# A four-layer graph network on one core: index layout, x loads, the place of the pair sums, ScalarE's order at batch norms and copies, and two basis groups moved

## The chip, the cores and the metric

The kernel runs on one core of one Trainium2 chip. The metric is the device time of one execution in microseconds (us). Lower is better. The core has TensorE (PE, matrix products into PSUM), VectorE (DVE), ScalarE (ACT), GpSimd (POOL) and SyncE (SP, here only a queue that issues DMAs). Each engine works through its own instructions in order, and waits on semaphores for what others produce.

## The reference, cut to what matters

Four graph layers follow one another on x (512 nodes, 512 features); each adds its output to x, and reads relu(layernorm(x)). All use one edge list of 16896 edges (`dst`, `src`), the last also a type of 0 or 1 for each edge.

```python
# layer 0: attention over the adjacency, 8 heads of 64, softmax over the heads for each pair of nodes
q, k, v = x @ Wq + bq, x @ Wk + bk, x @ Wv + bv              # each as (N, H, HEAD)
scores = einsum('nhd,mhd->nhm', q, k) / sqrt(HEAD)
scores = where(adj[:, None, :] == 0, -1e9, scores)
attn = softmax(scores, axis=1)                                # over the heads
out = einsum('nhm,mhd->nhd', attn, v) @ Wo + bo
h1 = layer_norm(x + out); y = layer_norm(h1 + relu(h1 @ W1 + b1) @ W2 + b2)
# layer 1: x = prelu(x @ lin_W.T + lin_b), then twice
h = x + segment_sum(x[src], dst)
h = prelu(h @ conv_W1[l].T + conv_b1[l]) @ conv_W2[l].T + conv_b2[l]
x = relu((h - mean) * rsqrt(var + eps) * gamma[l] + beta[l])  # mean and var over the nodes
# layer 2: degree-normalised sum of neighbours, a product, leaky relu
# layer 3: twice: w[r] = sum_b att[r, b] * basis[b] (2 relations, 30 bases of 512x512);
#          sum over the edges of sigmoid(x_j @ gate[r]) * x_j @ w[r], plus x @ root + bias
```

## The kernel before

A 512x512 matrix lies as four tiles of 128 rows. The edge list is turned into dense 512x512 count matrices, one for each edge type (`Bc`), and all four layers work with these.

**The start** (L115 to L464). The three index vectors are read as rows of 128 edges (132 chunks): 128 rows into `idx` and the last four into `idx2`, six DMAs, for `dst` and `src` on SP's queue and for the type on ScalarE's. Two tiles of x are loaded on ScalarE's queue, two on SP's, then the weights Wq and Wk on SP. GpSimd meanwhile sets constants, and issues loads of its own (L148, L150, L179). VectorE casts the indices to `kn` (L393); TensorE transposes them into `key`, so that an edge chunk is a column (L395 to L398). `look_for_strays` (L404) tests whether any edge lies outside its expected range, and leaves a flag; a branch on the flag follows on all engines (L461, L462). The first layer norm is made by `moments` (bn_stats and bn_aggr on VectorE, L342) and `first_norm` (L378: a square root on ScalarE, a reciprocal and a product on VectorE, then a ReLU with bias and scale on ScalarE), for one tile after the other. `flip` (L329) transposes the result on TensorE, and ScalarE copies it out of PSUM.

**The counting loop** (L723 to L740) runs over 204 entries of (count tile, group, chunk). For each chunk `rows_of` makes two one-hot tiles, `hd` on VectorE and `hs` on ScalarE (L548) or VectorE (L550), up to seven chunks ahead; `count` is a small product into a count tile's two PSUM banks. At the end of each of the four count tiles `counted` (L560) moves the banks out with ScalarE and VectorE. Between the counts stand other steps of TensorE at places that a plan (L693 to L719) computes from the string `line`: `p` is half of a 4-matmul product of the q, k and v projections, `G` is a basis group, `s` and `S` are scores of the first two attention blocks, `=` is the head sums of block 0. The bias copy of a projection comes some entries after its second half (`waits`).

**The attention** (L744 to L758) runs over 8 blocks (two halves of the query nodes, four tiles of key nodes). For a block: `scores` (L616: products, and a copy by ScalarE into `sc`, 128x2048), `shift` (L633: maximum over the heads, subtraction, VectorE; then the exponential, ScalarE, in place), `pairs` (L646: a sum of two pairs of heads, VectorE, tile `z`), `sums` (L652: head sums by TensorE into one PSUM bank), `weigh` (L657: reciprocal and scaling, VectorE), `values` (L662: products with v). In pass j the loop scales block j, adds the pairs of j+1, makes scores and shift of j+2, the values of j-1 and the sums of j+1.

**The basis groups** (L227). Part of the sums over the bases of layer 3 is made on TensorE: 40 groups of four matrices, 8 instructions each, from weights loaded by SP. Two groups in the first half of the work, three in the second, fill a PSUM bank; ScalarE copies the bank and stores it (L249, L250). There is one such bank. The other bases are accumulated by VectorE (L268). The string `USES` (L34) gives the order in which the loads are used, P for TensorE and V for VectorE.

**Order.** An instruction wrapped in `on` (or `keep`) stays in program order with the others so wrapped on its engine. The others are placed by a list scheduler. All VectorE and ScalarE work of the attention loop is wrapped; in the batch norms it isn't.

**Layer 1** (L938 to L1006). After an aggregate over the edges, four banks are copied, two by ScalarE and two by VectorE (L949 to L954), and a product follows. For each of four tiles, the second product is moved out by ScalarE with a bias (L981), statistics and a ReLU follow (L982 to L989), and `settle` (L827) transposes the tile.

Of the kernel before, what the change touches and what calls it, by code (L numbers as in the profile page):

```python
# [17 lines left out]
P = 128  # L18
# [12 lines left out]
RB = 4  # L31
STEPS = 2
BANKS = 8
USES = "P" * 26 + "VPVVVPPPPVVVPPPVVVVPPPPPPVVVVVVVVVVVV"  # L34
FEW = 4095
LESS = 2.0 ** -12
GW = 32
# [37 lines left out]
def gnn_kernel(ctx: ExitStack, tc: tile.TileContext, out: bass.AP, a: dict):  # L75
# [36 lines left out]
    raw = ExitStack()  # L112
    rp = raw.enter_context(tc.tile_pool(name="raw", bufs=1))

    idx = rp.tile([P, 3, P], I32, name="idx")  # L115
    idx2 = rp.tile([NCH - P, 3, P], I32, name="idx2")
    for i, name in enumerate(("dst", "src", "edge_type_2")):
        queue = (nc.sync, nc.sync, nc.scalar)[i]
        queue.dma_start(idx[:, i, :], a[name][0:P * P].rearrange("(c p) -> c p", p=P))
        queue.dma_start(idx2[:, i, :], a[name][P * P:E].rearrange("(c p) -> c p", p=P))  # L120
    x = const.tile([P, T, D], F32, name="x")
    for t in range(T):
        (nc.scalar, nc.sync)[t // 2].dma_start(x[:, t, :], a["x"][t * P:(t + 1) * P, :])
    ident = const.tile([P, P], F32, name="ident")
    make_identity(nc, ident)

# [97 lines left out]
    wide2 = const.tile([P, 32], F32, name="wide2")  # L224
    sums = []

    def basis_step(n=1):  # L227
        for _ in range(n):
            if len(done) == len(loads):
                return  # L230
            l, n, g = loads[len(done)]
            done.append(n)
            assert USES[bases.at] == "P"
            t = bases.take()
            if g == 0:
                sums[:] = [pbas.tile([P, 512], F32, tag="bas", name="bas")]
            if g < STEPS:
                k, at = FULL * NQ, 32 - 2 * NQ * (g + 1)
                lhsT = wide[l][:k, at:at + 32]
            else:  # L240
                k = STEPS * HALF_OF * NQ
                lhsT = wide2[:k, :]
            for j in range(RB):
                tc.keep_in_program_order(nc.tensor.matmul(  # L244
                    sums[0][32 * j:32 * j + 32, :], lhsT=lhsT,
                    rhs=t[:k, j, :], start=(g == 0), stop=(g == STEPS + l - 1)))
            if g == STEPS + l - 1:
                o = spool.tile([P, 512], F32, tag="sums", name="sums")
                nc.scalar.copy(o, sums[0])  # L249
                nc.scalar.dma_start(summed[l][n], o)  # L250

    def wrel_load(l, r, t):
# [134 lines left out]
    key = ep.tile([P, 4, NCH], F32, name="key")  # L387
    p = ps()
    pk = p[:, :3 * NCH].rearrange("p (i c) -> p i c", i=3)
    for ix, c0 in ((idx, 0), (idx2, P)):  # L390
        n = ix.shape[0]
        kn = rp.tile([n, 3, P], F32, name=f"kn{c0}")
        on(nc.vector.tensor_copy(kn, ix))  # L393
        for i in range(3):
            on(nc.tensor.transpose(pk[:, i, c0:c0 + n], kn[:, i, :], ident[:n, :n]))  # L395
    moments(mv4[:, 0, :], x[:, 0, :], on)
    on(nc.vector.tensor_copy(key[:, 0:2, :], pk[:, 0:2, :]))
    on(nc.vector.tensor_scalar(key[:, 2, :], pk[:, 2, :], 0.0, LESS, op0=ALU.is_equal, op1=ALU.max))  # L398

    stray = ep.tile([P, NCH], F32, name="stray")  # L400
    flag = const.tile([1, 1], I32, name="flag")
# [2 lines left out]
    def look_for_strays():  # L404
        over = rp.tile([P, NCH], F32, name="over")
        on(nc.vector.tensor_tensor(stray, key[:, 0, :], lim[:, 0, :], ALU.is_lt))
        on(nc.vector.tensor_tensor(over, key[:, 0, :], lim[:, 1, :], ALU.is_ge))
        on(nc.vector.tensor_add(stray, stray, over))
        some = rp.tile([P, 1], F32, name="some")
        on(nc.vector.tensor_reduce(some, stray, AX.X, ALU.max))  # L410
        p = ps()
        on(nc.tensor.matmul(p[0:1, 0:1], lhsT=some, rhs=ones, start=True, stop=True))
        on(nc.vector.tensor_copy(iot, it))
        on(nc.vector.tensor_scalar(key[:, 3, :], key[:, 1, :], -1.0, 0.5, op0=ALU.mult, op1=ALU.add))
        on(nc.vector.tensor_copy(flag, p[0:1, 0:1]))
        first_norm(0)
        moments(mv4[:, 1, :], x[:, 1, :], on)

    strayed = dram.tile([2, P, T * N], F32, name="strayed")

# [31 lines left out]

    look_for_strays()
    for t in range(2, T):
        moments(mv4[:, t, :], x[:, t, :], on)
        first_norm(t - 1)
    first_norm(T - 1)
    far_off = const.tile([P, P], BF16, name="far_off")
    on(nc.vector.tensor_scalar(far_off, ident, FAR, None, op0=ALU.mult))
    nc.gpsimd.memset(apart, 1.0)  # L460
# [223 lines left out]
    def advance(gen, n=1):  # L684
        for _ in range(n):
# [9 lines left out]
    shifts = [blocks[i].shift(2) for i in range(2)]  # L695
    takes = {"p": (8, lambda: advance(proj)), "G": (4, basis_step), "s": (6, lambda: advance(early[0])),
             "S": (6, lambda: advance(early[1])), "=": (12, lambda: blocks[0].sums())}
    line = "pppppGpppGpppGppGpppGssppGpGSSppGpGppGG="
    FIRST = 9
    ends = [n for n in range(len(order) - 1) if order[n + 1][0] > order[n][0]]  # L700
    whole = sum(takes[i][0] for i in line)
# [1 line left out]
    waits = None  # L703
    for i, what in enumerate(line):
        at = max(at, FIRST + (len(order) - 2 - FIRST) * passes // whole)
        at = next((e for e in ends if e - 6 < at <= e), at)
        if waits is not None:
            plan.setdefault(min(waits, at), []).append(lambda: advance(proj))
            waits = None
# [2 lines left out]
        if what == "p":  # L712
            halves += 1
            if halves % 2 == 0:
                waits = at + 4
        if line[:i + 1].count(what) == 2 and what in "sS":
            for step in range(3):
                plan.setdefault(at + 7 * step + 7, []).append(lambda j="sS".index(what): advance(shifts[j]))
# [23 lines left out]
        pass  # L742
    aoT = big("B")
    for j, block in enumerate(blocks):  # L744
        block.weigh()
        if j + 1 < len(blocks):
            blocks[j + 1].pairs()
        if j + 2 < len(blocks):
            for _ in blocks[j + 2].scores():
                pass  # L750
        if j:
            blocks[j - 1].values()
        if j + 1 < len(blocks):
            basis_step(2 if j < 4 else 1)
            blocks[j + 1].sums()
        if j + 2 < len(blocks):
            for _ in blocks[j + 2].shift():
                pass  # L758
# [61 lines left out]
    def exactly(emit):  # L820
# [3 lines left out]
        with branch.Else():  # L824
            emit(f32, 0)

    def settle(l, h2T, m, xn):  # L827

        if l == 0:
# [43 lines left out]
    for t in range(T):  # L873
# [8 lines left out]
        if t > 1:  # L882
            flip(y, t - 2, hT)
        transposed(t)
        basis_step(t % 2)
        if t < 2:
            advance(more)

# [49 lines left out]
    for l in range(2):  # L938
# [14 lines left out]
            else:  # L953
                on(nc.scalar.copy(aT[:, m, :], p))  # L954
        if l == 0:
            basis_step(2)
            advance(more, 3)
        else:
            advance(more, 2)
# [16 lines left out]
        for m in range(T):  # L976
            p = ps()
            product(p, [(w[:, k, ts(m)], h1T[:, k, :]) for k in range(T)])
            at = CB2 + T * l + m
            v = h2T[:, m, :]  # L980
            nc.scalar.activation(v, p, AF.Identity, bias=cols[:, at:at + 1])  # L981
            mean, rstd = stats(v)  # L982
            at = T * l + m
            sg = stat("sg")
            nc.vector.tensor_mul(sg, rstd, cols[:, GAM + at:GAM + at + 1])
            off = stat("off")
            nc.vector.tensor_mul(off, mean, sg)
            nc.vector.tensor_sub(off, cols[:, BET + at:BET + at + 1], off)
            nc.scalar.activation(v, v, AF.Relu, bias=off, scale=sg)  # L989
            if m > 1:  # L990
                settle(l, h2T, m - 2, xn)
            if m < 2:
                advance(more)
        if l == 0:
            basis_step(1)
            settle(l, h2T, 2, xn)
            basis_step(2)
            settle(l, h2T, 3, xn)
        else:
            basis_step(1)  # L1000
            settle(l, h2T, 2, xn)
            basis_step(1)
            settle(l, h2T, 3, xn)
            basis_step(1)
            gates = gate_rows(1, [apart.bitcast(F32).rearrange("p t n -> p (t n)")[:, N * r:N * r + N] for r in range(2)])
            next(gates)  # L1006
# [186 lines left out]
```

## Time and profile before

| | us |
|---|---|
| median of 3 runs | 525.57 (525.04 to 527.74) |
| profiled execution, its own time | 527.14 |
| its span | 525.3 |
| TensorE busy | 485.9 |
| VectorE busy | 402.4 |
| ScalarE busy | 196.6 |
| GpSimd busy | 37.4 |
| mean granted TensorE clock | 0.997 of full speed |
| first projection product (L479) starts | 21.17 |
| last values product (L670) ends | 189.4 |

An instruction's line in the profile is given as L and a number, that of the code above. A row of a timeline gives start, duration, engine, line, operation, output and input, a number of instructions, and in brackets the idle time of the engine before it and what ended it. A row of waits gives who waited for whom, the total in us, how often, and the longest. A row of windows gives a stretch and its length, the busy time of PE, weight loads, DVE, ACT and POOL with the numbers of instructions, the granted clock, the share of the DMA engines' time, and GB/s. Busy times of matmuls are modelled from their starts.

### The profile page before, as it was taken

Reading aid. Unit: us, or ns where it says so; the run is one execution under the profiler, and the core shown is the slowest. Engines: PE = TensorE matmul, PEld = TensorE weight load, DVE = VectorE, ACT = ScalarE, POOL = GpSimd, SP = SyncE. Lnnn points to the kernel's source line nnn. Section 1 sums busy time; section 2 is a strip of 40 time slices with the busy share of each in tenths; the row PEclk is TensorE's granted clock in tenths of the full one; section 3 lists DMA queues with packets and bytes.
Section 4 is the critical chain, followed back from the end, with each engine's and each line's share of the span. In section 5 each row is a group of like instructions: output and inputs, shape, how many; then the busy total and the mean of one; then the engine's idle time right before and its main releaser. Section 6 shows DMA issues by size and latency. Waiting matters only on the chain.

```text
span 525.3 us, 5734 instructions
## 1 busy us (share of the span) xinstructions
PE 485.9 (93%) x2014; PEld 248.7 (47%) x2014; DVE 402.4 (77%) x746; ACT 196.6 (37%) x318; POOL 37.4 (7%) x81
## 2 busy tenths in 40 slices
PE   1798999888999899999999899899699999999996
PEld 1333333334555545784444444644454475446642
DVE  6755477969889778999985597688649999999611
ACT  2786768753354212222421215224623610114000
POOL 6000000000000011110040000000010000000000
PEclk9999999998999999999999999999999999999999
DMA  7998777499896749959571794966932994530011
GB/s 229 267 226 220 189 188 171 118 257 230 208 213 165 156 94 262 288 186 238 128 234 67 243 233 121 365 152 169 251 70 80 305 274 167 171 145 2 0 41 41
DMA packets 43033, 94.06 MB, mean 179 GB/s; under 512 B 2124, under 2 KB 2520, under 8 KB 43000
## 3 DMA queue, kind: packets, MB, share of 16 engines
q1 hardware_dynamic: 34544, 67.77, 48.6%
q0 software_dynamic: 5712, 21.07, 13.9%
q10 hardware_dynamic: 2744, 4.79, 2.8%
q8 instruction: 20, 0.33, 0.3%
q14 instruction: 13, 0.11, 0.1%
HBM read 88.38 MB, written 5.24 MB: 178 GB/s over the span
## 4 chain that ended last, share of the span: by engine, by line
PE 66%; DVE 21%; ACT 9%; POOL 2%; issue 2%; ACTq 0%; POOLq 0%
PE pr L320 15%; PE acc L1101 10%; PE pg L320 7%; PE bas L244 4%; DVE wrel L268 4%; PE ps L479 4%; PE ps L655 4%; PE acc L1067 3%; PE ao L557 3%; ACT hs L548 2%; DVE st L344 2%; PE ps L492 2%; PE ao L670 2%; PE acc L918 2%; DVE sc L660 2%; PE psc L628 2%
## 5 line engine op out<-in xcount | busy, mean ns | idle before, releaser
L268 DVE SCALAR_TENSOR_TENSOR wrel<-basis,scal,wrel 128x1024 f32<-128x1024 f32 x60 | 74.2, 1283 | 1.9 <-DMA basis<-in_basis 1.9
L548 ACT ACTIVATE hs<-iot,key 128x512 f16<-128x512 f16 x75 | 49.1, 713 | 9.9 <-PE ao L557 8.2
L544 DVE TENSOR_SCALAR hd<-iot,key 128x32 f16<-128x32 f16 (+1 forms) x132 | 33.7, 294 | 21.6 <-PE ao L557 21.4
L244 PE MATMUL bas<-basis,wide 120*32 120x512 f32 (+1 forms) x320 | 43.3, 600 | 2.9 <-ACT sums L249 2.1
L268 DVE SCALAR_TENSOR_TENSOR w<-basis,scal,w 128x1024 f32<-128x1024 f32 x32 | 39.4, 1283 | 0.0
L557 PE MATMUL ao<-hs,hd 128*32 128x512 f16 x204 | 26.1, 395 | 3.5 <-DVE Bc L566 1.6
L479 PE MATMUL ps<-bigB,w 128*128 128x512 f32 x56 | 27.8, 618 | 1.0 <-ACT bigD L482 0.6
L352 ACT ACTIVATE sd<-mv,eps 128x1 f32<-128x1 f32 x28 | 8.1, 294 | 53.0 <-DVE mv L345 52.0
L644 ACT ACTIVATE sc<-sc 128x2048 f32<-128x2048 f32 (+1 forms) x10 | 15.7, 1566 | 22.4 <-DVE sc L643 22.3
L320 PE MATMUL pr<-bigE,w 128*128 128x512 f32 x48 | 21.4, 595 | 1.7 <-ACT bigE L954 1.7
L1149 DVE TENSOR_TENSOR u<-acc,x 128x512 f32<-128x512 f32 x4 | 2.8, 693 | 23.5 <-PE acc L1101 23.5
L320 PE MATMUL pr<-bigD,w 128*128 128x256 f32 x88 | 20.2, 380 | 0.0
L550 DVE TENSOR_SCALAR hs<-iot,key 128x512 f16<-128x512 f16 x57 | 20.1, 360 | 0.0
L557 PEld LDWEIGHTS <-hd 128*32 128x32 f16 x204 | 6.2, 94 | 27.5 <-issue 19.4
L630 ACT COPY sc<-psc 128x1024 f32<-128x1024 f32 x16 | 16.1, 1008 | 8.1 <-PE psc L628 8.1
L659 DVE RECIPROCAL rec<-ps 128x256 f32<-128x256 f32 x8 | 14.1, 1757 | 6.4 <-PE ps L655 6.4
L643 DVE TENSOR_TENSOR sc<-sc,half 128x2048 f32<-128x2048 f32 (+1 forms) x10 | 18.6, 1865 | 0.2
L660 DVE TENSOR_TENSOR sc<-sc,rec 128x2048 f32<-128x2048 f32 x8 | 18.3, 2292 | 0.3
L628 PE MATMUL psc<-bigC,bigD 64*128 64x256 f32 x128 | 18.2, 402 | 0.0
L320 PEld LDWEIGHTS pr<-bigD,w 128*128 128x128 f32 x88 | 16.6, 190 | 3.0 <-ACT bigE L863 0.8
L320 PE MATMUL pr<-w,bigE 128*128 128x512 f32 x40 | 17.8, 592 | 0.0
L492 PE MATMUL ps<-w,bigB 128*128 128x512 f32 x32 | 15.9, 618 | 2.0 <-DVE bigE L495 2.0
(312 smaller groups left out, 957.4 us busy)
## 6 DMA issues: line engine op xcount, KB each, us to landing
basis<-in_basis SPq DMA_DIRECT2D x32, 960.0 KB, 9.2
basis<-in_basis SPq DMA_DIRECT2D x23, 1024.0 KB, 9.6
basis<-in_basis SPq DMA_DIRECT2D x16, 448.0 KB
summed<-sums ACTq DMA_DIRECT2D x16, 256.0 KB, 7.2
w<-in_W POOLq DMA_DIRECT2D x4, 1024.0 KB, 7.0
row<-in_rows POOLq DMA_DIRECT2D x12, 256.0 KB, 9.6
wrel<-summed POOLq DMA_DIRECT2D x4, 512.0 KB, 7.9
w<-in_conv_W1T POOLq DMA_DIRECT2D x2, 1024.0 KB, 5.7
```

Of the source, the lines that this page charges most:

```text
L244: tc.keep_in_program_order(nc.tensor.matmul(sums[0][32 * j:32 * j + 32, :], lhsT=lhsT, rhs=t[:k, j, :], start=(g == 0), stop=(g == STEPS + ...
L268: on(nc.vector.scalar_tensor_tensor(to[r][:, i:i + 2, :], t[:, i:i + 2, :], scal[:, at:at + 1], to[r][:, i:i + 2, :], op0=ALU.mult, op1=AL ...
L320: nc.tensor.matmul(p, lhsT=lhsT, rhs=rhs, start=(i == 0), stop=(i == len(pairs) - 1))
L479: on(nc.tensor.matmul(p, lhsT=w[:, k, ts(m)], rhs=made["hT"][:, k, :], start=(k == 0), stop=(k == T - 1)))
L492: on(nc.tensor.matmul(p, lhsT=made["hT"][:, k, ts(t)], rhs=w[:, k, :], start=(k == 0), stop=(k == T - 1)))
L544: keep(nc.vector.tensor_scalar(hd[:, :w], iot[:, GW * groups_of[c][0]:GW * groups_of[c][0] + w], key[:, 0, c:c + 1], key[:, 2, c:c + 1], o ...
L548: keep(nc.scalar.activation(hs, iot, AF.Sign, bias=key[:, 3, c:c + 1]))
L557: keep(nc.tensor.matmul(cnt[b][GW * (g % T):GW * (g % T) + GW, :], lhsT=hd[:, at:at + GW], rhs=hs, start=(c == in_bank[g][b][0]), stop=(c ...
L628: on(nc.tensor.matmul(p[:, b, i, :], lhsT=kT[bs, 2 * q + i, ts(self.mt)], rhs=qT[bs, 2 * q + i, self.ns], start=False, stop=(i == 1)))
L655: on(nc.tensor.matmul(self.total, lhsT=ident, rhs=part, start=(j == 0), stop=(j == len(self.parts) - 1)))
L660: on(nc.vector.tensor_mul(self.sc, self.sc, rec[:, None, :].to_broadcast([P, H, NH])))
L1101: nc.tensor.matmul(self.out[t], lhsT=self.uT[r][:, k, ts(t)], rhs=wrel[r][:, k, :], start=False, stop=(r == 1 and k == T - 1))
```

## The change

The indices are read as 66 rows of 256 edges, three DMAs; the cast is made for one vector at a time, and each is transposed in two halves, to the even and the odd chunks. All of x is loaded on SP, ahead of the weights. Statistics and norm of tiles 0 and 1 come ahead of the stray test, statistics of tiles 2 and 3 inside it. In the plan, the snap to the end of a count tile reaches six entries to both sides, the bias copy comes two entries after its product, and the string's last part is changed. In the attention loop `pairs` of the next block comes ahead of `weigh`, and the second group of a pass ahead of the values. At the batch norms, the bias copy of tile m is kept ahead of the ReLU of tile m-1; at the first copy one group is issued, with its bank's copy kept in order. One group each is taken from the feed-forward's last tile and from that copy, and put at the end of each batch norm. `USES` follows.

```diff
-USES = "P" * 26 + "VPVVVPPPPVVVPPPVVVVPPPPPPVVVVVVVVVVVV"
+USES = "P" * 26 + "VPVVVPPVVVPPPPVVVVPPPPPPPVVVVVVVVVVVV"
...
-    idx = rp.tile([P, 3, P], I32, name="idx")
-    idx2 = rp.tile([NCH - P, 3, P], I32, name="idx2")
+    idx = rp.tile([NCH // 2, 3, 2 * P], I32, name="idx")
...
-        queue.dma_start(idx[:, i, :], a[name][0:P * P].rearrange("(c p) -> c p", p=P))
-        queue.dma_start(idx2[:, i, :], a[name][P * P:E].rearrange("(c p) -> c p", p=P))
+        queue.dma_start(idx[:, i, :], a[name].rearrange("(c p) -> c p", p=2 * P))
...
-        (nc.scalar, nc.sync)[t // 2].dma_start(x[:, t, :], a["x"][t * P:(t + 1) * P, :])
+        nc.sync.dma_start(x[:, t, :], a["x"][t * P:(t + 1) * P, :])
...
-    def basis_step(n=1):
+    def basis_step(n=1, keep=lambda ins: ins):
...
-                nc.scalar.copy(o, sums[0])
+                keep(nc.scalar.copy(o, sums[0]))
...
-    for ix, c0 in ((idx, 0), (idx2, P)):
-        n = ix.shape[0]
-        kn = rp.tile([n, 3, P], F32, name=f"kn{c0}")
-        on(nc.vector.tensor_copy(kn, ix))
-        for i in range(3):
-            on(nc.tensor.transpose(pk[:, i, c0:c0 + n], kn[:, i, :], ident[:n, :n]))
+    kn = rp.tile([NCH // 2, 3, 2 * P], F32, name="kn")
+    for i in range(3):
+        on(nc.vector.tensor_copy(kn[:, i, :], idx[:, i, :]))
+        for j in range(2):
+            on(nc.tensor.transpose(pk[:, i, j:NCH:2], kn[:, i, ts(j)], ident[:NCH // 2, :NCH // 2]))
...
+    moments(mv4[:, 1, :], x[:, 1, :], on)
+    for t in range(2):
+        first_norm(t)
...
+        moments(mv4[:, 2, :], x[:, 2, :], on)
         on(nc.vector.tensor_copy(flag, p[0:1, 0:1]))
-        first_norm(0)
-        moments(mv4[:, 1, :], x[:, 1, :], on)
+        moments(mv4[:, 3, :], x[:, 3, :], on)
...
     for t in range(2, T):
-        moments(mv4[:, t, :], x[:, t, :], on)
-        first_norm(t - 1)
-    first_norm(T - 1)
+        first_norm(t)
...
-    line = "pppppGpppGpppGppGpppGssppGpGSSppGpGppGG="
+    line = "pppppGpppGpppGppGpppGssppGpGSSpGpGpGppG="
...
-        at = next((e for e in ends if e - 6 < at <= e), at)
+        at = next((e for e in ends if abs(at - e) < 7), at)
...
-                waits = at + 4
+                waits = at + 2
...
     for j, block in enumerate(blocks):
-        block.weigh()
         if j + 1 < len(blocks):
             blocks[j + 1].pairs()
+        block.weigh()
...
+        if j in (1, 2, 3, 5):
+            basis_step()
         if j:
             blocks[j - 1].values()
         if j + 1 < len(blocks):
-            basis_step(2 if j < 4 else 1)
+            basis_step()
             blocks[j + 1].sums()
...
+    def normed(l, h2T, m, mv):
+        at = T * l + m
+        sd = stat("sd")
+        nc.scalar.activation(sd, mv[:, 1:2], AF.Sqrt, bias=eps)
+        sg = stat("sg")
+        nc.vector.reciprocal(sg, sd)
+        nc.vector.tensor_mul(sg, sg, cols[:, GAM + at:GAM + at + 1])
+        off = stat("off")
+        nc.vector.tensor_mul(off, mv[:, 0:1], sg)
+        nc.vector.tensor_sub(off, cols[:, BET + at:BET + at + 1], off)
+        on(nc.scalar.activation(h2T[:, m, :], h2T[:, m, :], AF.Relu, bias=off, scale=sg))
...
-        basis_step(t % 2)
+        basis_step(t == 1)
...
-            basis_step(2)
+            basis_step(1, on)
...
-            v = h2T[:, m, :]
-            nc.scalar.activation(v, p, AF.Identity, bias=cols[:, at:at + 1])
-            mean, rstd = stats(v)
...
-            nc.scalar.activation(v, v, AF.Relu, bias=off, scale=sg)
+            on(nc.scalar.activation(h2T[:, m, :], p, AF.Identity, bias=cols[:, at:at + 1]))
+            if m:
+                normed(l, h2T, m - 1, moment)
+            moment = stat("mv", 2)
+            moments(moment, h2T[:, m, :])
...
-        if l == 0:
-            basis_step(1)
-            settle(l, h2T, 2, xn)
-            basis_step(2)
-            settle(l, h2T, 3, xn)
-        else:
-            basis_step(1)
-            settle(l, h2T, 2, xn)
-            basis_step(1)
-            settle(l, h2T, 3, xn)
+        basis_step(1)
+        normed(l, h2T, 3, moment)
+        settle(l, h2T, 2, xn)
+        basis_step(3 - l)
+        settle(l, h2T, 3, xn)
+        if l:
             basis_step(1)
```

More of the change, by code (lines that the diff above doesn't have):

```diff
@@ L979, in gnn_kernel @@
             at = CB2 + T * l + m
-            v = h2T[:, m, :]
-            nc.scalar.activation(v, p, AF.Identity, bias=cols[:, at:at + 1])
-            mean, rstd = stats(v)
[L983 to L989, printed above, removed]
+            on(nc.scalar.activation(h2T[:, m, :], p, AF.Identity, bias=cols[:, at:at + 1]))
[3 more added lines that the diff above has]
+            moments(moment, h2T[:, m, :])
             if m > 1:
```

## The prediction, made before the change was run

> **What bounds the kernel now.** I read the page first, then TensorE's waits, then the timeline engine by engine at each place the diff touches, then busy time by window. The page's first part:
>
> ```profile
> PE 485.9 (93%) x2014; PEld 248.7 (47%) x2014; DVE 402.4 (77%) x746; ACT 196.6 (37%) x318; POOL 37.4 (7%) x81
> ```
>
> TensorE is busy for 485.9 of 525.3 us, and no matmul is removed, so all that can be won is in its 39.4 us of idle time. About 13 us of that is the start, 4 us the last four output rows (26.21 busy in the last 30.30 us). The rest is short waits. From TensorE's waits (us in total, times, longest), those that the change can touch:
>
> ```profile
> PE psc L395 <- DVE kn L393: 7.3, 1, 7.3
> PE ps L655 <- DVE z L649: 3.3, 2, 1.9
> PE pg L333 <- ACT bigD L989: 3.3, 2, 1.7
> ...
> PE ps L492 <- DVE bigE L495: 2.0, 2, 1.3
> ...
> PE pr L320 <- ACT bigE L954: 1.7, 1, 1.7
> PE ao L557 <- DVE Bc L566: 1.6, 2, 1.1
> ```
>
> Against these stand the places where VectorE, not TensorE, is the limit. A block of the attention in steady state, from VectorE's timeline (start, us, operation):
>
> ```profile
> 172.07 2.29 DVE L643 TENSOR_TENSOR sc<-sc,half 128x2048 f32<-128x2048 f32 x1
> 174.38 1.76 DVE L659 RECIPROCAL rec<-ps 128x256 f32<-128x256 f32 x1
> 176.17 2.29 DVE L660 TENSOR_TENSOR sc<-sc,rec 128x2048 f32<-128x2048 f32 x1
> 178.38 0.69 DVE L649 TENSOR_TENSOR z<-sc 128x512 f32<-128x512 f32 x1
> ```
>
> and ScalarE beside it:
>
> ```profile
> 174.45 1.91 ACT L644 ACTIVATE sc<-sc 128x2048 f32<-128x2048 f32 x1 [5.31 <-DVE sc L643]
> ```
>
> The reader is to see that the exponential (1.91 us) lies under the reciprocal and the scaling of the block before (174.38 to 178.4). The pair sum z needs it, and comes after both, so it finds it done.
>
> **Part 1, the start.** First the index load and VectorE's cast of it, beside GpSimd:
>
> ```profile
> L393 DVE CAST kn<-idx x2: 354/1357/2360, 4.7 to 7.0; 128x384 f32<-128x384 int32 x1, 4x384 f32<-4x384 int32 x1
> ```
> ```profile
> 4.41 0.58 POOL L152 IOTA it<- 128x512 int32 x1
> 4.91 0.22 POOL L155 MEMSET zero<- 128x128 f16 x1
> 5.06 2.16 POOL L179 DMA_DIRECT2D row<-in_rows  x4
> 7.22 1.91 POOL L460 MEMSET apart<- 128x2048 bf16 x1
> ```
>
> The large cast takes 2360 ns for 384 elements; L413 casts 512 in 420 ns. It ends at 7.11, when GpSimd's run of an iota, a memset and four DMA issues ends. The Trainium skill ("SBUF — State Buffer", Who interferes with whom) says that a copy or cast in a two-port mode and a GpSimd instruction exclude each other, and that whoever starts first holds the ports for that instruction. By the rule the cast loses at most the iota (to 4.99) and ends near 5.4; the row shows it losing to six instructions in a row. For the change: three index DMAs instead of six save three issues (0.33 to 0.58 us each), so the indices land perhaps 0.8 us earlier, near 3.9. By the rule three casts of 256 elements (0.2 to 0.3 us each, from L413's rate) are over by 5. By the row they sit until 7.2 again and end at 7.5 instead of 7.36. I take the row. 66 index rows and the x tiles behind one another on SP cost nothing in it: all have landed by 7 in either order (0.76 of the DMA engines' time to 12 us), and the weights behind them are first read at 21.2.
>
> From 7.5 VectorE has, ahead of the last norm: four statistics pairs (0.85 each, 3.4), two key copies (0.55), four reciprocal and bias pairs (0.33 each, 1.3), one new stall of 0.4 where tile 1's reciprocal waits for the square root (0.29), and the stray test with its cast and flag (9.12 to 10.66, 1.54): 7.2, so 14.7. The flag comes about 2.5 us later; queued behind it are the branch on all engines and SP's next basis loads, first needed at 35. The last ReLU (0.81) ends at 15.5 against 16.92 now, because ScalarE, idle from 8.5 to 11.2 today, gets the first two earlier. Four transposes and copies follow in both, then the first projection at 21.17. Gain 1.5. Ends: 0 (the counts' one-hots, behind more VectorE work, come last) and 4 (by the rule).
>
> **Part 2, the counting loop (20 to 108).** The arithmetic of the plan gives new places for TensorE's steps. At the ends of count tiles 0 and 1 (entries 49 and 101) a projection half moves from entry 51 (or stays next to 105), so that two stand at the end: 3.84 us of cover instead of 1.92 for the evacuation. The waits there are 1.11 at 42.4, and 0.50 and 0.20 at 66.5. Bias copies come two entries after their product instead of four: waits of 0.24, 0.24 and 0.35 (L482) and 0.70 at 81.6 (L495). Sum 3.3. ScalarE or VectorE may now sit on a product not ready, with one-hots queued behind; they run up to seven chunks ahead, which covers a product of 1.92. In the last tile VectorE is busy for 11.24 of 12 us (96 to 108), so the 1.33 wait at 94 should stay, though the two groups at entries 187 and 190 now lie further apart (0.70 at 107.4). I take 2.5; ends 0.5 and 4.
>
> **Part 3, pair sums ahead of the scaling.** VectorE's order in block j becomes: z of j+1, reciprocal and scaling of j, maxima and subtraction of j+2. All are kept in program order. Now z of j+2 stands directly behind the subtraction, and the exponential between them is uncovered: 0.04 + 1.91 + 0.04, about 1.98 us of VectorE idle in each of blocks 2 to 7. A block's VectorE work is z 0.61, reciprocal 1.79, scaling 2.21, maxima 1.25 + 0.73 + 0.46, subtraction 2.29: 9.34 (as in 166.82 to 176.17: 9.35). It becomes 11.33. TensorE has 10.05 a block with two basis groups, 9.06 with one, so it can't hide that. Block 1 was finished early; its z starts at 114.95. Then z of block 2 at 126.28, block 7 at 182.93, reciprocal 6 to 185.33. The one-bank total of block 7 waits for that: 2.86 of sums to 188.25, reciprocal 7, scaling to 192.35 (now 186.10). TensorE's last values end at 195.8, against 189.4: 6.3 later. What is saved is counted in this: the 1.46 and 1.86 waits for z, VectorE's 6.35 of waits for sums, and a clock drop:
>
> ```profile
> 121.00:122.00 1.00, 1.00 (x4) 0.73 (x4) 0.93 (x3) 0.00 (x0) 0.00 (x0) 0.50 1.01 209
> ```
>
> The granted clock (third number from the end) fell to 0.50 after 2.2 us idle (0.70 and 1.46) between 116.5 and 119.7, and the sums behind took 4.54 instead of 2.79. The skill ("TensorE: Matmul & The Clock Gate", Part 1) has the clock drop after an idle window of about 3.4 us, so it would leave it full in the new blocks' gaps of 1.3 to 2.3; by the row, 1.75 may be lost after a gap that is not whole. It would matter only ahead of block 7, so I count nothing, and 1.75 in the upper end. The moved basis groups (second ones ahead of the values) are as many as before and hide in TensorE's slack. Cost 6.3; ends 5 and 8.
>
> **Part 4, copies and batch norms.** At the layer-0 copy ScalarE's sums copy stands ahead of the aggregate's copies:
>
> ```profile
> 294.80 0.58 ACT L249 COPY sums<-bas 128x512 f32<-128x512 f32 x1 [4.58 <-PE bas L244]
> ...
> 295.78 1.07 ACT L954 COPY bigE<-acc 128x512 f32<-128x512 f32 x2 [0.40 <-ACT sums L249]
> ```
>
> Now one group is issued there and in order: the four copies end near 293.9 (VectorE's last at 293.6), and the product starts there instead of 296.42: 2.5, of which 0.99 is the group moved away. At the batch norms, ReLU of tile 2 holds the identity of tile 3:
>
> ```profile
> 325.11 0.81 ACT L989 ACTIVATE bigD<-bigD,off,sg 128x512 f32<-128x512 f32 x1 [0.88 <-DVE off L988]
> 325.83 0.67 ACT L981 ACTIVATE bigD<-pg,cols 128x512 f32<-128x512 f32 x1
> ```
>
> With the identity first (324.5) the last ReLU ends about 2 us earlier (1.2 in layer 1, where the wait before the identity is shorter). TensorE's gaps there, 1.60 and 1.69, take one moved group each (0.99, and in layer 0 up to 0.70 for the sums bank), so the last transposes come only 0.1 and 0.6 earlier. The group taken from the feed-forward's last tile gains nothing: at 276.6 TensorE waits for VectorE's chain (F L936, 277.2) anyway; 0.99 at best. Small statistics are as many as before. Gain 3.2; ends 1.5 and 4.5. The order of V and P loads follows the groups.
>
> **Sum and rivals.** -1.5 - 2.5 + 6.3 - 3.2 = -0.9. The profiled execution took 527.14 (span 525.3 and 1.8 around it), so 526.2 on its own scale; the median shown is 1.57 lower: 524.7.
>
> *Likeliest, 0.36:* the gains and the uncovered exponential cancel, 522.9 to 528.2, at 524.7. About 0.5% (2.6 us) is what a measurement of this kernel can tell from no change.
>
> *Faster, 0.32:* the casts get in before GpSimd's run (start 4), the loop gives 3.5, the feed-forward's group counts (4.2): -11.7 + 6.3 = -5.4, 520.2. For it: GpSimd's four row issues start only at 5.06. Against it: 2360 ns in the row.
>
> *Slower, 0.32:* the uncovered exponential in lines 643 to 649, priced at 6.3, or 8 with one clock drop ahead of block 7. It decides once the other parts together give less than 3.7; with half of what I expect of them (3.6) and 7.5 for it, +3.9: 529.5. For it: VectorE's order is fixed, and waits removed one by one are often replaced. That the order isn't kept I give no chance.
>
> Range 520 to 530: it leaves out about 0.2, the ends of both outer cases.
>
> **What would show it.** After the change z L649 should wait for sc L644, six times about 2 us, and a block should last 11.3; waits of TensorE for z should be few. The casts' durations tell rule from row. L954 should start before 293.5 on today's scale, and L981 ahead of L989. If VectorE has no wait for the exponential, part 3 is wrong and the result is near 518; if the casts end by 5, part 1 is.

## The result, and the profile after

The changed kernel takes 544.46 us (median of 4 runs, 543.56 to 547.14) against 525.31 for the kernel before beside it (523.6 to 527.74): a ratio of 1.037, 95% interval 1.031 to 1.043. The prediction was 524.7 with a range to 530, so it missed by 20. The profiled execution took 543.56 (span 541.7, against 525.3); its mean granted clock is 0.983 against 0.997. Line numbers after the change are lower by one or two up to the attention (L390 was L393, L242 was L244, L648 was L649), and higher by 14 or so at layer 1's copy (L968 was L954).

The first line of the page, engines' busy time:

```profile
PE 493.9 (91%) x2014; PEld 251.1 (46%) x2014; DVE 400.7 (74%) x747; ACT 195.5 (36%) x318; POOL 37.7 (7%) x81
```

TensorE runs the same 2014 products and is busy 8.0 longer: no product was added, so they ran slower, at the lower clock (by the two means, 9.2 of the span was withheld after and 1.6 before, 7.6 more, a part of it in idle time). It is also idle 8.4 longer. TensorE's waits (total, times, longest) say for what:

```profile
PE ps L654 <- DVE rec L658: 13.0, 7, 5.5
PE bas L242 <- DMA basis<-in_basis: 11.3, 2, 5.8
PE psc L392 <- DVE kn L390: 4.3, 1, 4.3
...
PE ao L556 <- DVE hs L549: 3.1, 2, 2.8
PE ao L556 <- ACT hs L547: 2.8, 7, 0.7
```

The first two rows have no counterpart before. The first is the attention, the second is new: twice TensorE stands still for a basis load. The third is the start (7.3 before). The last two are what came in the place of the waits at the start and in the counting loop.

Starts of the same work in both traces, and what each stretch lost:

| | before | after | stretch, after minus before |
|---|---|---|---|
| first projection | 21.17 | 19.87 | -1.3 |
| VectorE's attention loop starts (reciprocal of block 0 before, pair sum of block 1 after) | 114.95 | 111.74 | -1.9 |
| last values product ends | 189.47 | 193.79 | +7.5 |
| first product behind the layer-0 copy | 296.42 | 297.80 | -2.9 |
| aggregate behind the first batch norm | 330.51 | 339.04 | +7.2 |
| product behind it | 337.87 | 348.87 | +2.5 |
| aggregate of layer 2 | 375.97 | 389.78 | +2.8 |
| product behind it | 387.42 | 403.68 | +2.4 |
| end | 525.3 | 541.7 | +0.1 |

All that was won (6.1) is given back in the attention, and 14.9 more is lost from the first batch norm to layer 2.

**The attention.** VectorE (start, duration, operation):

```profile
168.34 0.69 DVE L648 TENSOR_TENSOR z<-sc 128x512 f32<-128x512 f32 x1 [1.98 <-ACT sc L643]
168.95 1.75 DVE L658 RECIPROCAL rec<-ps 128x256 f32<-128x256 f32 x1
170.73 2.29 DVE L659 TENSOR_TENSOR sc<-sc,rec 128x2048 f32<-128x2048 f32 x1
...
175.38 2.29 DVE L642 TENSOR_TENSOR sc<-sc,half 128x2048 f32<-128x2048 f32 x1
179.64 0.69 DVE L648 TENSOR_TENSOR z<-sc 128x512 f32<-128x512 f32 x1 [1.97 <-ACT sc L643]
```

From z to z it is 11.30, and VectorE waits 1.97 for the exponential, six times (11.9 in all): both as predicted. TensorE then waits 5.53 ahead of block 7's sums, and runs the first 2.8 us of them (182.06 to 184.9) at a clock of 0.50.

**The first batch norm.** TensorE (in brackets the idle time before, and what ended it):

```profile
326.34 1.06 PE L242 MATMUL bas<-basis,wide 120*32 120x512 f32 x8
...
331.08 0.66 PE L331 MATMUL pg<-ident,bigD 128*128 128x128 f32 x4 [0.21 <-ACT bigD L839]
337.19 1.92 PE L242 MATMUL bas<-basis,wide 120*32 120x512 f32 x2 [5.46 <-DMA basis<-in_basis]
339.04 0.80 PE L318 MATMUL acc<-R,bigA 128*128 128x512 f32 x1
...
347.88 1.06 PE L242 MATMUL bas<-basis,wide 120*32 120x512 f32 x6
```

This is the batch norm's fourth group. Two of its eight instructions stand ahead of the aggregate (337.19), the other six behind it (347.88). The aggregate needs nothing of the group, but TensorE works in order: before, the aggregate started 0.41 after the last transposes (330.10, 330.51), and here 7.96 after (331.08, 339.04). SP issued its load here, and waited for this:

```profile
327.47 0.33 SPq L198 DMA_DIRECT2D basis<-in_basis  x1
```
```profile
SPq L198 <- PE bas L242: 11.8, 1, 11.8
```

SP stood 11.8 (315.6 to 327.4) until the first group of this batch norm (326.34, 1.06 long) was done, then issued, and the matrix was used 9.7 after. The loads have four slots. At that time two held the second and third group, one the first group, and the fourth a matrix that VectorE had added in three of its four parts. Its last addition stands far behind in VectorE's order:

```profile
313.94 2.48 DVE L266 SCALAR_TENSOR_TENSOR wrel<-basis,scal,wrel 128x1024 f32<-128x1024 f32 x2
317.15 1.25 DVE L266 SCALAR_TENSOR_TENSOR wrel<-basis,scal,wrel 128x1024 f32<-128x1024 f32 x1
321.40 1.25 DVE L266 SCALAR_TENSOR_TENSOR wrel<-basis,scal,wrel 128x1024 f32<-128x1024 f32 x1
333.00 1.28 DVE L266 SCALAR_TENSOR_TENSOR wrel<-basis,scal,wrel 128x1024 f32<-128x1024 f32 x1
```

The first of these two additions at 313.94 ends the matrix ahead; the second and the next two are three parts of this one, and the fourth comes at 333.00. So three groups can be ready at a batch norm, not four. Before the change there were three groups at each, loaded ahead in three slots. The second batch norm repeats it (5.80).

Behind the wait the clock is low. Stretches of 1 us; the third number from the end is the granted clock, the last GB/s:

```profile
338.00:339.00 1.00, 1.00 (x2) 0.00 (x0) 0.00 (x0) 0.00 (x0) 0.00 (x0) 0.50 1.04 391
...
341.00:342.00 1.00, 1.00 (x4) 0.81 (x3) 1.00 (x2) 0.00 (x0) 0.00 (x0) 0.54 0.71 256
342.00:343.00 1.00, 1.00 (x5) 0.78 (x5) 0.61 (x1) 0.49 (x1) 0.00 (x0) 1.00 0.09 20
```

From the aggregate's start to the next product it is 9.83, against 7.36 before: the +2.5 of the table. Of this, 1.5 is the aggregate at the low clock (8.84 until 347.88), and 0.99 the six instructions of the fourth group. The +2.4 in layer 2 divides in the same way.

**The start.** The three casts, after (shortest, median, longest; from and to), and then the large cast with the unchanged start in another execution, that of the kernel before with only the pair sums moved:

```profile
L390 DVE CAST kn<-idx x3: 314/315/919, 3.2 to 4.3; 66x256 f32<-66x256 int32 x3
```
```profile
4.09 0.47 DVE L393 CAST kn<-idx 128x384 f32<-128x384 int32 x1 [3.19 <-DMA idx<-in_src]
```

The casts end at 4.6, ahead of GpSimd's iota (4.92). And the old cast, 2360 ns in the profile of before, takes 470 where the indices land at 4.09 instead of 4.75. Of the five kernels profiled with the old start, four show the late cast (it starts at 4.56 to 4.83) and this one the early. In the eleven with the new start the casts begin at 3.13 to 3.38.

### The profile page after: what moved, and what is told of

It reads as the page before. It is cut to its first block, busy times and chain, and to the rows that moved or that the text cites. A ratio compares the mean times of both kernels' runs of the same rounds, so it can differ in the third digit from the quotient of the medians.

```text
span 541.7 us, 5727 instructions
## 1 busy us (share of the span) xinstructions
PE 493.9 (91%) x2014; PEld 251.1 (46%) x2014; DVE 400.7 (74%) x747; ACT 195.5 (36%) x318; POOL 37.7 (7%) x81
## 4 chain that ended last, share of the span: by engine, by line
PE 65%; DVE 20%; ACT 7%; DMA 3%; issue 2%; ACTq 0%; SPq 0%; DVEq 0%
PE pr L318 18%; PE acc L1106 10%; PE pg L318 10%; PE ps L478 4%; PE bas L242 4%; DMA basis<-in_basis 3%; PE acc L932 3%; DVE sc L642 3%; ACT sc L643 3%; DVE sc L659 3%; PE acc L1072 3%; PE ao L556 3%; ACT hs L547 2%; DVE rec L658 2%; PE acc L318 2%; DVE wrel L266 2%
## 5 line engine op out<-in xcount | busy, mean ns | idle before, releaser
L242 PE MATMUL bas<-basis,wide 120*32 120x512 f32 (+1 forms) x320 | 47.5, 606 | 12.2 <-DMA basis<-in_basis 11.3
L556 PE MATMUL ao<-hs,hd 128*32 128x512 f16 x204 | 27.5, 400 | 6.1 <-DVE hs L549 3.1
L350 ACT ACTIVATE sd<-mv,eps 128x1 f32<-128x1 f32 x20 | 5.8, 294 | 47.6 <-DVE mv L343 46.6
L654 PE MATMUL ps<-z,ident 128*128 128x256 f32 x32 | 10.0, 438 | 13.5 <-DVE rec L658 13.0
L242 PEld LDWEIGHTS bas<-basis,wide 120*32 120x32 f32 (+1 forms) x320 | 9.0, 109 | 25.9 <-issue 16.4
L478 PEld LDWEIGHTS ps<-bigB,w 128*128 128x128 f32 x56 | 9.7, 189 | 14.9 <-issue 11.1
```

Of the source, the lines that this page charges most:

```text
L242: tc.keep_in_program_order(nc.tensor.matmul(sums[0][32 * j:32 * j + 32, :], lhsT=lhsT, rhs=t[:k, j, :], start=(g == 0), stop=(g == STEPS + ...
L478: on(nc.tensor.matmul(p, lhsT=w[:, k, ts(m)], rhs=made["hT"][:, k, :], start=(k == 0), stop=(k == T - 1)))
L556: keep(nc.tensor.matmul(cnt[b][GW * (g % T):GW * (g % T) + GW, :], lhsT=hd[:, at:at + GW], rhs=hs, start=(c == in_bank[g][b][0]), stop=(c ...
```

## The experiments

Each kernel was timed in 5 rounds with the kernel before beside it on the same chip. The medians of before were 525.0 (first four kernels), 525.1, 525.9 and 526.1 (last two), so kernels of different groups are compared by their ratios. Differences in us are those of the medians; by the ratios they come out up to 1 us otherwise. Theory: two independent losses, uncovered exponential and late fourth loads. Rivals for the second: ScalarE's kept order at the batch norms, or the later attention, makes the loads late.

**1. Groups put back in the changed kernel.**

```diff
-USES = "P" * 26 + "VPVVVPPVVVPPPPVVVVPPPPPPPVVVVVVVVVVVV"
+USES = "P" * 26 + "VPVVVPPPPVVVPPPVVVVPPPPPPVVVVVVVVVVVV"
...
-        basis_step(t == 1)
+        basis_step(t % 2)
...
-            basis_step(1, on)
+            basis_step(2, on)
...
-        basis_step(3 - l)
+        basis_step(2 - l)
```

> The changed kernel with only the groups put back: the order string of the loads, the group at the feed-forward's last tile, the second group at the layer-0 copy and three groups at each batch norm as before; ScalarE's kept order at copies and batch norms stays. Slot theory (the fourth load for TensorE in a row must wait until VectorE has finished the last matrix ahead of it, and lands 9 us later): TensorE's wait for basis (11.3 in two times) is gone, the clock stays full there, and the time falls by about 14 of the 14.9 us that were lost behind the layer-0 copy, less 1 for the group back at that copy: 530 (528 to 532). Rival (the kept order of identity, ReLU and statistics on ScalarE delays the batch norms, and the load is only late because all is): 541 or more, the waits for basis stay in some form. Rival (the late attention collides with the stream of loads, whichever order it has): 538 to 544.

Measured 530.72, ratio 1.0119 (1.0089 to 1.0148). No row of waits for a basis load is left at the batch norms, and TensorE's only wait from 320 to 345 is the old gap:

```profile
PE pg L331 <- ACT bigD L839: 1.6, 1, 1.6
```

So the groups' place costs 13.7 (13.1 by the ratios), with ScalarE's order and the late attention unchanged: both rivals fall.

**2. Scaling put back ahead of the pair sums.**

```diff
+        block.weigh()
         if j + 1 < len(blocks):
             blocks[j + 1].pairs()
-        block.weigh()
```

> The changed kernel with only the scaling back ahead of the pair sums. Uncovered-exponential theory: VectorE's six waits for the exponential go, a block lasts 9.4 to 10 instead of 11.3, the values end 7.5 earlier (186 instead of 193.7), and the loss at the batch norms is untouched: 537 (535 to 539). Rival (the late attention is what makes the loads late at the batch norms): the waits for basis shrink too, 525 to 530.

Measured 536.48, 1.0236 (1.0199 to 1.0274). The values end at 184.97 instead of 193.79, and the wait for basis is still 11.6 in two times. The losses don't depend on one another.

**3. Both put back**, the edits of 1 and 2 together.

> The changed kernel with both put back: what stays is the start, the plan of the counting loop, and ScalarE's order at copies and batch norms. If the two losses are the only ones and independent: 544.5 - 14 - 7.5 = 523 (520 to 524), which is under the kernel before (525.3), by the 3.2 us that the start and the counting loop showed at the first attention block and what the ScalarE order gives at the copy. If these gains are given back later: 525 to 526.

Measured 523.34, 0.9967 (0.9950 to 0.9984): under the kernel before by 1.7. From 544.46, the single edits took 13.7 and 8.0, both together 21.1 (13.1, 7.0 and 21.1 by the ratios), so they add up. TensorE now waits 3.23 for z of block 1 (1.46 before): the new plan makes TensorE's work ahead of it end earlier, and VectorE's scaling stands in between.

**4. Two VectorE matrices loaded and not added**, those of uses 35 and 43 (places in `USES`, counted from 0), ahead of the two runs of four groups.

```diff
+                    if use not in (35, 43):
                         on(nc.vector.scalar_tensor_tensor(to[r][:, i:i + 2, :], ...
```

> The changed kernel, all groups where the change put them, but the last VectorE matrix ahead of each run of four TensorE groups (uses 35 and 43) is loaded and not added; this leaves out two of the matrices' sums on VectorE (8 of its accumulations), so the output lacks two bases. Slot theory: the slot is free once it is loaded, so the fourth load is not late, TensorE's waits for basis go, and the time is 529 to 531, as with the groups back. Rival (four groups at a batch norm are simply too much on TensorE's path, or the kept order on ScalarE is the cost): 540 or more, since the groups and the order are all still there. VectorE's saved accumulations alone, where VectorE is not the limit, are worth under 2 us.

Measured 529.12, 1.0096 (1.0065 to 1.0127). All four groups stand at the batch norms, with no wait for a load. The expectation's wording was not right, though: it has the late load wait for VectorE's last addition. The trace of the changed kernel shows it released by TensorE's first group, because VectorE's slot comes free later still (333.00). Since leaving additions out is also less work, experiment 9 repeats this with all work kept.

**5. Pair sums first in the first pass alone**, groups back.

```diff
-        if j + 1 < len(blocks):
+        if j == 0:
+            blocks[1].pairs()
+        block.weigh()
+        if 0 < j < len(blocks) - 1:
             blocks[j + 1].pairs()
-        block.weigh()
```

> Groups back, and the pair sums ahead of the scaling only in the first pass, where block 1's exponential was finished long before; in the other passes the scaling comes first again. Uncovered-exponential theory: no exponential is uncovered, and TensorE's wait for z of block 1 (3.2 us, with the low clock behind it about 4 more at the next sums) goes: 3 us under the kernel with both put back, about 520 (519 to 522). If the order in that one pass only moves the wait to the next block: 523.

Measured 519.72 (519.4 to 520.0), 0.990 (0.987 to 0.993): 5.4 under its own runs of before, and 24.7 under the changed kernel. It beats both kernels. VectorE waits for no exponential, and the values end at 183.59 (185.70 with the scaling first in every pass).

**6. One of the two groups put back**, so that the first batch norm has three groups and the second four.

```diff
-USES = "P" * 26 + "VPVVVPPVVVPPPPVVVVPPPPPPPVVVVVVVVVVVV"
+USES = "P" * 26 + "VPVVVPPPVVVPPPVVVVPPPPPPPVVVVVVVVVVVV"
...
-            basis_step(1, on)
+            basis_step(2, on)
...
-        basis_step(3 - l)
+        basis_step(2)
```

> The changed kernel with one of the two moved groups put back (the layer-0 copy has two groups and the first batch norm three again; the feed-forward's last group is still at the end of the second batch norm), so the runs of loads for TensorE behind VectorE's matrices are three long at the first batch norm and four at the second. Slot theory: one wait for basis of about 5.8 us, at the second batch norm only, and none at the first: 537 (535 to 539), half-way between the changed kernel and the one with both groups back. If what matters is how much later the whole is, or the number of groups at a batch norm: both waits shrink together, or both go.

Measured 536.15, 1.0205 (1.0162 to 1.0248), and the row of waits stands once:

```profile
PE bas L242 <- DMA basis<-in_basis: 6.2, 1, 6.2
```

The wait goes with the fourth group, place by place.

**7. The two losses alone, on the kernel before.** First the pair sums alone (the edit of experiment 2 the other way round), then the groups and their order string alone (that of experiment 1 the other way round, in the old batch norm).

> The kernel before, with only the pair sums put ahead of the scaling. Uncovered-exponential theory, as between the two kernels with the groups back (530.7 and 523.3): +7, 532 (531 to 534). The prediction said +6.3 for this part alone.

> The kernel before, with only the two groups moved to the ends of the batch norms and the order string that goes with it (ScalarE's order, start, plan and attention as before). Slot theory: two waits for basis at the batch norms, 10 to 13 us more: 537 (535 to 539). Rival (the waits need ScalarE's kept order or the later attention as well): 523 to 526.

Pair sums: 535.06, 1.0203 (1.0167 to 1.0239), that is +10.0; its profiled span is 7.3 over that of before (532.6 against 525.3), though its profile has the early cast and starts 1.2 earlier. The six waits for the exponential are the same 11.9. From the first projection to the end of the values it takes 8.2 longer than before (176.5 against 168.3), and experiment 1 takes 8.5 longer than experiment 3 (174.3 against 165.8). So in the profiles the loss is much the same on both kernels; why the medians are 10.0 apart here and 7.4 there is not shown, and their intervals, near 2 us to each side, hardly tell the two apart. Groups: 538.63, 1.0257 (1.0221 to 1.0293), with this row:

```profile
PE bas L244 <- DMA basis<-in_basis: 12.2, 2, 6.1
```

So each loss comes with its own edit, on either kernel.

**8. The smaller parts.** First the kernel before with the pair sums first in the first pass alone. Then the kernel of experiment 5 with one part of the change undone: the counting loop's plan (the string, the snap, the bias copy's place), ScalarE's order at copy and batch norms, or the start. One piece of each of these three edits:

```diff
-                waits = at + 2
+                waits = at + 4
```
```diff
-            on(nc.scalar.activation(h2T[:, m, :], p, AF.Identity, bias=cols[:, at:at + 1]))
-            if m:
-                normed(l, h2T, m - 1, moment)
+            v = h2T[:, m, :]
+            nc.scalar.activation(v, p, AF.Identity, bias=cols[:, at:at + 1])
+            mean, rstd = stats(v)
```
```diff
-        nc.sync.dma_start(x[:, t, :], a["x"][t * P:(t + 1) * P, :])
+        (nc.scalar, nc.sync)[t // 2].dma_start(x[:, t, :], a["x"][t * P:(t + 1) * P, :])
```

> The kernel before, with the pair sums ahead of the scaling in the first pass alone. Theory: no exponential is uncovered, and TensorE's wait of 1.46 for z of block 1 and the low clock behind it (1.75) go: 3 under the kernel before, 522 (521.5 to 523.5). If the wait is replaced by another (the one bank of the group sums, 0.7 ahead of it): 524 to 525.

> The kernel with the groups back and the pair sums first in the first pass alone (519.7), with the counting loop's plan of before. The counting loop's part, which the trace gave about 1.9: 521.6 (521 to 522.5). The prediction's term for it was 2.5. If the plan gave nothing that lasts: 519.7.

> The same kernel (519.7), with ScalarE's order at the layer-0 copy and the batch norms of before. From the last values to the first product behind the copy it took 105.2 against 107.0 in the kernel before, and the two batch norms 0.2 and 0.3 less: 2.2 in all, so 522 (521 to 523). If that came from elsewhere: 519.7.

> The same kernel (519.7), with the start of before (index layout, x on two queues, order of statistics and norms). Two profiles of kernels with that start had the first projection at 21.17 (casts from 4.75, 2.63 long) and a third at 19.94 (cast from 4.09, 0.47 long), against 19.87 with the new start. Theory: the indices land either ahead of GpSimd's run or behind it, so the executions spread over 1.3: 519.7 to 521, with a wider spread than that of the new start. Theory of a fixed cost: all at 521.

| | us | ratio to before (95%) | what the profile shows |
|---|---|---|---|
| before, pair sums first once | 523.85 | 0.9973 (0.9958 to 0.9987) | values end 186.17 (189.47) |
| experiment 5 | 519.72 | 0.9900 (0.9869 to 0.9932) | |
| plan back | 520.67 | 0.9914 (0.9892 to 0.9935) | first projection to end of values 164.6 (163.7) |
| order back | 521.75 | 0.9925 (0.9903 to 0.9947) | end of values to product behind the copy 106.9 (105.2) |
| start back | 519.78 | 0.9888 (0.9865 to 0.9911) | first projection 21.17 (19.86), span 518.9 (517.9) |

The intervals of the last four overlap, so the times don't settle the parts. In the profiles the order is worth 2.1 (1.7 at the copy), as expected; the plan 0.9 at the end of the values, instead of 1.9; and the start 1.3 at the first projection and 1.0 at the end, in an execution with the late cast. The 0.9 hides a chance of the clock. From the first projection to block 7's pair sum the plan is worth 2.5 (151.0 against 153.5). Then TensorE waits 1.85 for that pair sum in experiment 5 and 1.86 with the plan back; behind the first the clock is 0.50 for 3.4 us (172.4 to 175.8), behind the second it stays full, so the rest takes 12.8 against 11.1. In time the start gave nothing that was measured in the median; with the old start the times spread over 518.24 to 520.85, with the new over 519.4 to 520.0, which fits the theory of a landing ahead of GpSimd's run or behind it.

**9. Additions earlier, nothing left out.** All groups stay where the change put them; VectorE finishes the matrices of uses 35 and 43 ahead of the batch norm.

```diff
-            advance(more, 2)
+            advance(more, 5 if m == 3 else 2)
...
-            if m < 2:
-                advance(more)
```

> The changed kernel with all its groups where it put them, nothing left out; only VectorE's additions stand earlier: three more behind the last tile of each layer-1 block's first product, none in its batch norm (one more in sum), so that the matrix of use 35 (and 43) is finished about 10 us before the fourth group. Account A (the fourth of the four slots is held by the half-added matrix, whose last addition stands behind the batch norm, and the fourth group's load must wait for the first group's slot): both waits for basis go, 529 to 531, as with the groups back or with the two matrices unused. Account B (the waits need fewer groups or less work at the batch norm; leaving the additions out helped only as less work): 540 or more.

> The same, with the pair sums ahead of the scaling in the first pass alone: the whole change with its two losses removed. Account A: the moved groups now fill the two gaps of 1.4 at the batch norms, and one group is gone from the layer-0 copy, so 1 under the kernel with the groups back (519.7): 518.7 (518 to 519.7). Account B: 533 or more.

Measured 530.73, 1.0115 (1.0085 to 1.0145), and 520.90, 0.9913 (0.9888 to 0.9938). In the first the half-added matrix is done at 319.60, the fourth group's load is issued at 319.62, and the group no longer waits for it. TensorE:

```profile
328.13 1.06 PE L242 MATMUL bas<-basis,wide 112*32 112x512 f32 x8
329.90 1.92 PE L242 MATMUL bas<-basis,wide 120*32 120x512 f32 x16 [0.71 <-ACT sums L247]
331.75 0.66 PE L331 MATMUL pg<-ident,bigD 128*128 128x128 f32 x4
332.16 0.47 PE L318 MATMUL acc<-R,bigA 128*128 128x512 f32 x1
```

Account A holds: the slot held by the half-added matrix made the load late. The second kernel was expected at 518.7 and is no better than experiment 5. From the product behind the copy to layer 2's aggregate it takes 81.3 (287.55 to 368.86) against 79.1. So the moved groups, even without the late load, cost at the batch norms (2.2) more than was won at the copy (1.2 earlier). Its trace has TensorE waits at the batch norms that experiment 5 has not: 0.70 for the one bank, and 0.39, 0.40 and 0.18 for ReLUs; those of the first tiles come late because their statistics stand behind VectorE's additions (in layer 0 these last from 303.68 to 309.75, and the statistics start at 309.66). Against this, the two gaps of 1.45 and 1.40 are down to 0 and 0.43. The shares of the groups and of the additions' new place were not told apart; moving the groups paid nothing here.

## Why the prediction was wrong

- **The step that failed** is the last sentence of part 4, "The order of V and P loads follows the groups": the sum gave it no term. It cost 13.7 in the changed kernel and 13.5 on the kernel before (experiments 1 and 7). Part 4 costed the moved groups' instructions on TensorE (0.99 each) and not their loads: how many groups can be in slots at a batch norm, and what frees the next. The trace of before had it: 9.2 from issue to landing, and the load behind each group at the first batch norm issued only when that group was done (326.08, behind a group that ended at 326.02).
- **Part 1** chose the row (2360 ns) over the skill's rule on shared ports ("SBUF — State Buffer", Who interferes with whom). The casts went by the rule: over at 4.6, where the forecast had 7.5, and none kept until 7.2. The row told of indices that land behind the start of GpSimd's iota (4.41), as four of the five profiles with the old start do; the new ones landed at 3.2, not near 3.9. The gain was still 1.3, near the 1.5 taken, but by luck: the casts ended 2.9 earlier than forecast, and new waits took that back (2.81 of TensorE for a one-hot of VectorE). Against the one execution with the early cast the gain is 0.07 (19.87 against 19.94).
- **Part 2** gave 1.9 by the start of VectorE's attention loop against 2.5. In the kernel with both losses removed the plan is worth 2.5 up to block 7, and a clock drop then takes 1.7 of it back (experiment 8).
- **Part 3** had the mechanism right: six waits of 1.98, a block of 11.30 (predicted 11.33). Size 7.5 against 6.3. The clock drop ahead of block 7, which the likeliest case left out, happened: its sums started at 182.06 and took 4.25 instead of 2.86, that is 1.4. The sum had put their start at 185.33, but from a block 1 that starts 3.2 later. On the clock the row was a better guide than the rule beside it: gaps of 1.85 to 1.96 were followed by a drop in ten profiles of sixteen (see the end).
- **Part 4**, the copy: from the groups' start to the product it took 3.62 before (292.80 to 296.42) and 1.00 after (296.80 to 297.80), so it gained 2.6 (2.5 predicted), 1.7 from the order and 0.9 from the group moved away. The batch norms missed on two counts. First, the order that the part counted on is not in the trace: the ReLU of tile 2 still runs ahead of the identity of tile 3, as before the change. Why the kept order did not bring this about is open.

```profile
326.16 0.81 ACT L839 ACTIVATE bigD<-bigD,off,sg 128x512 f32<-128x512 f32 x1 [1.27 <-DVE off L838]
326.88 0.67 ACT L994 ACTIVATE bigD<-pg,cols 128x512 f32<-128x512 f32 x1
```

With the groups back (experiment 5) TensorE's gaps are still 1.45 and 1.40, against 1.60 and 1.69, so the last ReLU came nowhere near 2 us earlier, and the order gave 0.4 at both batch norms together. Second, the gaps did not take the moved groups free of cost: with no load late (experiment 9, second kernel) the way from the product behind the copy to layer 2's aggregate is 81.3, against 79.55 before, 1.8 longer where the forecast had 0.7 less.

- **Rivals.** The slower case named only the exponential, at 529.5; with the groups back, that loss alone gives 530.72. So this rival was right for its part, and no case held the loads.

## What to carry to other kernels

When a step that consumes a streamed load is moved, count slots, not only its instructions: which tiles are held at that moment (half-used ones too), when the next slot comes free, and whether issue plus landing (here 9.7) fits into what is left. An engine that has used three quarters of a buffer holds it whole; finishing it a few us earlier can be worth more than the step that was moved. Before trusting a duration in a row, see whether it depends on what landed just ahead of it.

## What was not expected of the hardware

- After 5.46 us without work, TensorE was granted 0.50 of its clock for 4.7 us more (337.2 to 341.9), so that the wait for a load cost about 2.4, half of that, beyond itself. Shorter waits could be enough: each of the sixteen profiles has one gap of 1.85 to 1.96 late in the attention, and behind it the clock was 0.50 for 3.4 us in ten of them (158.8 to 162.2 in experiment 1) and stayed full in six, the changed kernel's among them (1.95). Such a drop lengthens the span by 1.7, more than most of the smaller parts are worth. After 3.23 idle (experiment 3) the sums took 4.6 instead of 2.86, so 1.7 was lost there.
- A load of 960 KB took 9.7 from issue to use while the core's DMA engines were busy 0.86 and 1.03 of the time and moved 272 and 265 GB/s (two stretches from 327.4 to 337.2): other loads were under way beside it.
- The same cast of 128x384 took 470 ns or 2360 ns, by whether the indices landed at 4.09 or 4.75. Beside the new casts (from 3.20 on), GpSimd's three operations at 2.75 took 1.69 instead of 1.12.
